# Middle attention by halves of four heads: scores and turned probabilities in alternation

## Chip, cores and metric

The kernel runs on one core of one Trainium2 chip. The metric is the device time of one execution in microseconds; the time of a kernel is the median of several runs, and one further execution is profiled.

## What is computed

The reference is a two-layer network on a batch of 2 sequences of 1024 tokens with 256 channels. Each layer is a sum of conditioned blocks: an adapter and a recurrent mixing block, a mixture of experts, then an attention whose output conditions a second, local attention, and a gated feed-forward block. The change touches only the attention in the middle, `_L1_cond_ref`:

```python
Q, K, V = (proj(Wq, bq), proj(Wk, bk), proj(Wv, bv))      # 16 heads of 16 channels
s_scores = jnp.einsum('bhsd,bhskd->bhsk', Q, Kg) * scale  # Kg: K at 32 listed keys
s_scores = jnp.where(prior_index_mask[:Ss][None, None], s_scores, -inf)
sparse_out = jnp.einsum('bhsk,bhskd->bhsd', jax.nn.softmax(s_scores, axis=-1), Vg)
...
return out @ Wo.T + bo
```

Every query looks at 32 listed keys, which may repeat. All listed keys lie among the first 256, so the kernel computes full scores against 256 keys and adds the logarithm of how often each key is listed (`lc`), which comes to the same softmax.

## The kernel before

The code is written with a tile framework: the program says which engine computes what on which tile; the framework puts in the waits, hands out the buffers of each pool and sets the order in every engine's queue. In that order the place of a statement in the program is its priority, and an instruction that lacks a buffer lets later ones that are ready go first. So queues are not strictly in program order.

The middle attention is `cond1_near` (L1014). After the projections (`cond1_project`) it has 32 items: 2 batches, 4 pairs of query blocks of 128, 4 groups `g` of 4 heads. A group's four heads lie in the four strips of 32 partitions, 16 rows each. An item goes through three steps:

- `scores` (L1037): 8 matmuls (4 heads x 2 query blocks, row block outside, head inside) into four PSUM banks `ps0` to `ps3`, one for each head. Then for each head and block a reduction on VectorE (L1056) that adds `lc`, negates, writes `pe` to SBUF and leaves the row minimum in `nm`, and an exponential on ScalarE (L1066).
- `turn` (L1069): for each head four transposes on TensorE (L1075) into one of two PSUM banks `ptp`, and a copy to `pt` in SBUF: heads 0 and 2 on VectorE (L1078), heads 1 and 3 on ScalarE (L1080).
- `values` (L1086): first one step that is left over from earlier items (`later`: dividing by the softmax's sum and turning back, L981 to L993, or a piece of the output projection, L1008; two of them when more than four are left), then 8 matmuls (L1097) into bank `po` and a copy `aU` on ScalarE (L1104).

`staggered` (L70) runs the steps as a pipeline: in round i, `scores` of item i, `turn` of item i-1, `values` of item i-2. The eight PSUM banks are all in use: four `ps`, two `ptp`, one `po`, one `pa` for the left-over steps. In float32 a matmul is two passes, that is two weight loads and two matmul records in the profile, except for a transpose, which is one.

When the stage ends, the last output steps run, a branch on the data follows that leaves out `cond1_any`, and then the second attention loads its weights (`load_attn1`, L1229).

Of the kernel before, what the change touches and what calls it, by code (L numbers as in the profile page):

```python
# [9 lines left out]
F32 = mybir.dt.float32  # L10
# [8 lines left out]
P = 128  # L19
# [10 lines left out]
NEAR = 256  # L30
# [39 lines left out]
def staggered(items, *steps):  # L70

    for i in range(len(items) + len(steps) - 1):
        for j, step in enumerate(steps):
            if 0 <= i - j < len(items):
                step(items[i - j])
# [796 lines left out]
def combine(k, x, ys):  # L872

    nc, tc = k.nc, k.tc
    with tc.tile_pool(name="mog", bufs=4) as gp, tc.tile_pool(name="moq", bufs=2, space=PSUM) as pp:
        for b4 in range(NCK):
            po = [pp.tile([P, CK], F32, name=f"po{c}") for c in range(2)]
            for j in range(4):
                blk = b4 * 4 + j
                g = []  # L880
                for kk in range(2):
                    t = gp.tile([P, C], F32, name=f"g{kk}")
                    i = kk * NBLK + blk
                    nc.gpsimd.indirect_dma_start(
                        out=t[:],
                        out_offset=None,
                        in_=ys[:],
                        in_offset=bass.IndirectOffsetOnAxis(ap=k.gi[:, i : i + 1], axis=0),
                    )
                    g.append(t)  # L890
                o = gp.tile([P, C], F32, name="o")
                nc.vector.tensor_scalar_mul(o, g[0], k.cw[:, 0, blk : blk + 1])
                nc.vector.scalar_tensor_tensor(o, g[1], k.cw[:, 1, blk : blk + 1], o, ALU.mult, ALU.add)
                for c in range(2):
                    nc.tensor.transpose(po[c][:, j * P : (j + 1) * P], o[:, c * P : (c + 1) * P], k.ident)
            for c in range(2):
                ts = slice(b4 * CK, (b4 + 1) * CK)
                nc.vector.tensor_add(x[:, c, ts], x[:, c, ts], po[c])
# [73 lines left out]
def cond1_divide(k, sp, tp, aU, aT, qs):  # L972


    nc = k.nc
    a = sp.tile([P, 16, 16], F32, name="a")

    def divide():
        pa = tp.tile([P, 4, P], F32, name="pa")
        for g in range(4):  # L980
            nc.tensor.transpose(pa[:, g, :], aU[g], k.ident)  # L981
        p4 = pa.rearrange("p g (r d) -> p (g r) d", d=32)
        rd = sp.tile([P, 16], F32, name="rd")
        nc.vector.reciprocal(rd, p4[:, :, 16])
        nc.vector.tensor_mul(a, p4[:, :, 0:16], rd.unsqueeze(2).to_broadcast([P, 16, 16]))

    def back():
        pb = tp.tile([P, 4, P], F32, name="pa")
        a2 = a.rearrange("p h d -> p (h d)")
        for c in range(2):  # L990
            nc.tensor.transpose(pb[:, c, :], a2[:, c * P : (c + 1) * P], k.ident)
        for c in range(2):
            nc.vector.tensor_scalar_add(aT[:, c, qs], pb[:, c, :], k.vec("bv", c))  # L993

    return [divide, back]
# [18 lines left out]
def cond1_near(k, x, o, ys):  # L1014

    nc, tc = k.nc, k.tc
    nkb = NEAR // P  # L1020
    with tc.tile_pool(name="l1r", bufs=2) as rp:
        its = []
        with tc.tile_pool(name="l1a", bufs=2, space=PSUM) as pp:
            combine(k, x, ys)
            for b in range(B):
                qT = rp.tile([P, 4, S], F32, name="qT")
                kT = rp.tile([P, 4, NEAR], F32, name="kT")
                v = rp.tile([P, nkb, 16, 32], F32, name="v")
                aT = rp.tile([P, 2, S], F32, name="aT")
                cond1_project(k, x, b, pp, qT, kT, v, NEAR)  # L1030
                its += [dict(at=(b, q0, g), qT=qT, kT=kT, v=v, aT=aT) for q0 in range(0, 8, 2) for g in range(4)]
        with (
            tc.tile_pool(name="l1s", bufs=2) as sp,
            tc.tile_pool(name="l1p", bufs=1, space=PSUM) as pp,
        ):

            def scores(it):  # L1037
                b, q0, g = it["at"]
                ps = [pp.tile([P, 2, NEAR], F32, name=f"ps{i}") for i in range(4)]
                for j in range(2):  # L1040
                    for i in range(4):
                        hp = slice(32 * i, 32 * i + 16)
                        nc.tensor.matmul(  # L1043
                            ps[i][:, j, :],
                            lhsT=it["qT"][hp, g, (q0 + j) * P : (q0 + j + 1) * P],
                            rhs=it["kT"][hp, g, :],
                            start=True,
                            stop=True,
                        )
                it["pe"] = []  # L1050
                for i in range(4):
                    pe = sp.tile([P, 2, NEAR], F32, name="pe", bufs=10)
                    for j in range(2):

                        nm = sp.tile([P, 1], F32, name="nm", bufs=4)
                        nc.vector.tensor_tensor_reduce(  # L1056
                            out=pe[:, j, :],
                            in0=ps[i][:, j, :],
                            in1=k.lc[:, q0 + j, :],
                            scale=-1.0,  # L1060
                            scalar=3.0e38,
                            op0=ALU.add,
                            op1=ALU.min,
                            accum_out=nm,
                        )
                        nc.scalar.activation(pe[:, j, :], pe[:, j, :], AF.Exp, bias=nm, scale=-1.0)  # L1066
                    it["pe"].append(pe)

            def turn(it):  # L1069
                it["pt"] = []  # L1070
                for i, pe in enumerate(it["pe"]):
                    ptp = pp.tile([P, nkb, 2, P], F32, name="ptp", bufs=2)
                    for j in range(2):
                        for kb in range(nkb):
                            nc.tensor.transpose(ptp[:, kb, j, :], pe[:, j, kb * P : (kb + 1) * P], k.ident)  # L1075
                    pt = sp.tile([P, nkb, 2, P], F32, name="pt", bufs=8)
                    if i % 2 == 0:
                        nc.vector.tensor_copy(pt, ptp)  # L1078
                    else:
                        nc.scalar.copy(pt, ptp)  # L1080
                    it["pt"].append(pt)

            state = {}
            later = []

            def values(it):  # L1086
                b, q0, g = it["at"]
                for _ in range(2 if len(later) > 4 else 1):
                    if later:
                        later.pop(0)()  # L1090
                if g == 0:
                    state["aU"] = sp.tile([P, 4, 2, P], F32, name="aU")
                aU = state["aU"]
                po = pp.tile([P, 2, P], F32, name="po")
                for kb in range(nkb):
                    for i in range(4):
                        nc.tensor.matmul(  # L1097
                            po[32 * i : 32 * i + 32],
                            lhsT=it["v"][:, kb, 4 * g + i, :],
                            rhs=it["pt"][i][:, kb],  # L1100
                            start=kb == 0,
                            stop=kb == nkb - 1,
                        )
                nc.scalar.copy(aU[:, g], po)  # L1104
                if g < 3:
                    return
                for j in range(2):
                    qs = slice((q0 + j) * P, (q0 + j + 1) * P)
                    later.extend(cond1_divide(k, sp, pp, [aU[:, n, j, :] for n in range(4)], it["aT"], qs))
                if q0 == 6:  # L1110
                    later.extend(cond1_output(k, b, o, it["aT"], pp, "pa"))

            staggered(its, scores, turn, values)
            for step in later:
                step()

# [553 lines left out]
```

## Time and profile before

| what | value |
|---|---|
| median of 3 runs | 1792.74 us (1789.65 to 1792.97) |
| the profiled execution | 1785.95 us, span 1784.2 us |
| mean granted TensorE clock | 0.942 |
| middle attention's items, first reduction to that of the last item | 807.17 to 997.20 us |
| L1043 matmuls, busy | 512 records, 61.5 us |
| L1097 matmuls, busy | 512 records, 36.1 us |
| VectorE's copies L1078 | 64, 44.1 us |
| ScalarE's copies L1080 | 64, 36.8 us |

PE is TensorE's matmuls, PEld its weight loads, DVE is VectorE, ACT is ScalarE. A line of groups gives source line, engine, operation, tiles written and read, shape and count; then busy time and mean nanoseconds of one; then the idle time of the engine just before these instructions and what ended it. A line of the timeline gives start and length in microseconds, and in brackets how long the engine was idle and what ended that. Matmuls overlap, so the busy time of a group counts overlapping ones once.

### The profile page before, as it was taken

The numbers are of one execution on the slowest core, as the hardware profiler recorded it, in microseconds if no ns is written. First come the engines' busy times: TensorE is split into PE (matmuls) and PEld (weight loads), VectorE is DVE, ScalarE is ACT, GpSimd is POOL, SyncE is SP. The second block draws the span as 40 slices with busy tenths as digits, with TensorE's granted clock in tenths as the row PEclk, the third lists the DMA queues.
The fourth block names the chain that finished last, engine by engine and source line by source line (L and its number), as shares of the span: only waits on it lengthen the run. The fifth ranks groups of instructions, "written<-read, shape, count | busy, mean of one in ns | idle before, by whom it ended". The sixth has DMA issues, their size and how long they took to land. (4 is left out here: it accounts for less than half of the span.)

```text
span 1784.2 us, 27948 instructions
## 1 busy us (share of the span) xinstructions
PE 1617.0 (91%) x11226; PEld 1037.3 (58%) x11226; DVE 905.1 (51%) x2589; ACT 656.2 (37%) x1450; POOL 173.0 (10%) x154
## 2 busy tenths in 40 slices
PE   6798788999599999689998879999999999999978
PEld 3345776456365665345655434676776467677546
DVE  2543746997300000246787512776872277687444
ACT  2123023344212222006777411553653155465321
POOL 0351420034100000420000010000000000000001
PEclk9699799999799999798999889999999999999969
DMA  8000006001334320210000020000000000000001
GB/s 310 0 1 1 3 3 205 1 24 48 122 103 130 106 87 31 65 42 1 1 2 1 2 97 0 1 2 1 2 1 1 0 1 1 1 1 2 1 0 48
DMA packets 38271, 64.66 MB, mean 36 GB/s; under 512 B 6897, under 2 KB 31729, under 8 KB 35185
## 3 DMA queue, kind: packets, MB, share of 16 engines
q1 hardware_dynamic: 33970, 52.25, 8.7%
q0 software_dynamic: 3072, 8.39, 1.5%
q8 instruction: 93, 1.52, 0.4%
q10 hardware_dynamic: 1088, 2.10, 0.4%
q14 instruction: 48, 0.39, 0.1%
HBM read 43.86 MB, written 18.87 MB: 35 GB/s over the span
## 5 line engine op out<-in xcount | busy, mean ns | idle before, releaser
L1382 ACT ACTIVATE pe<-pe,nm 128x449 f32<-128x449 f32 (+1 forms) x256 | 162.8, 638 | 237.0 <-DVE nm L1372 236.9
L1397 PE MATMUL pt<-ident,pe 128*128 128x128 f32 x960 | 132.3, 279 | 2.4 <-DVE pe L1387 0.8
L1372 DVE CUSTOM_DVE_ANT_0 pe<-ps,wb 128x449 f32<-128x449 f32 (+1 forms) x224 | 127.4, 605 | 5.7 <-PE ps L1366 4.8
L859 PE MATMUL po<-w,h 128*128 128x256 f32 x512 | 118.2, 384 | 0.0
L851 PE MATMUL ph<-xt,w 128*128 128x512 f32 x256 | 113.7, 602 | 2.3 <-ACT xt L846 2.3
L1364 PE MATMUL ps<-kT,qT 64*128 64x384 f32 (+1 forms) x512 | 113.1, 508 | 2.2 <-DVE nm L1372 1.1
L1066 ACT ACTIVATE pe<-pe,nm 128x256 f32<-128x256 f32 x256 | 105.8, 495 | 20.8 <-DVE nm L1056 20.7
L1415 PE MATMUL py<-ptt,v 128*64 128x128 f32 x1408 | 111.2, 282 | 0.0
L1397 PEld LDWEIGHTS pt<-ident,pe 128*128 128x128 f32 x960 | 103.1, 141 | 13.7 <-PE ps L1366 4.1
L859 PEld LDWEIGHTS po<-w,h 128*128 128x128 f32 x512 | 95.3, 190 | 23.4 <-issue 11.8
L1056 DVE CUSTOM_DVE_ANT_0 pe<-ps,lc 128x256 f32<-128x256 f32 x256 | 91.5, 420 | 32.3 <-PE ps L1043 31.4
L805 DVE SCALAR_TENSOR_TENSOR lc<-iok,idx,lc 128x256 f32<-128x256 f32 x248 | 105.7, 475 | 0.3
L1387 DVE TENSOR_SCALAR pe<-pe,rd 128x449 f32<-128x449 f32 (+1 forms) x256 | 100.4, 435 | 4.3
L838 DVE SCALAR_TENSOR_TENSOR xe<-more,xe 128x256 f32<-128x256 f32 x32 | 13.4, 479 | 170.0 <-DMA xe<-xs 159.4
L1075 PE MATMUL ptp<-ident,pe 128*128 128x128 f32 x512 | 80.3, 293 | 14.6 <-DVE pt L1078 11.0
L1415 PEld LDWEIGHTS py<-ptt,v 128*64 128x64 f32 x1408 | 77.2, 136 | 23.3 <-issue 21.2
L1400 DVE COPY ptt<-pt 128x512 f32<-128x512 f32 (+1 forms) x128 | 83.6, 653 | 4.5 <-PE pt L1397 3.9
L1075 PEld LDWEIGHTS ptp<-ident,pe 128*128 128x128 f32 x512 | 57.3, 146 | 47.2 <-DVE pt L1078 23.2
L851 PEld LDWEIGHTS ph<-xt,w 128*128 128x128 f32 x256 | 48.5, 193 | 62.2 <-issue 55.4
L1288 PE MATMUL pq<-c,w1ak 128*128 128x512 f32 x128 | 61.3, 623 | 13.7 <-DMA w1ak<-in_w1a 12.9
L1402 ACT COPY ptt<-pt 128x512 f32<-128x512 f32 (+1 forms) x128 | 68.7, 537 | 4.2 <-PE pt L1397 4.2
L854 ACT ACTIVATE h<-ph,vecs 128x512 f32<-128x512 f32 x64 | 44.0, 687 | 70.2 <-PE ph L851 70.2
(311 smaller groups left out, 2737.0 us busy)
## 6 DMA issues: line engine op xcount, KB each, us to landing
w<-in_mw SPq DMA_DIRECT2D x16, 1024.0 KB, 6.0
xs<-z SPq DMA_DIRECT2D x8, 1024.0 KB, 9.8
xe<-xs SPq DMA_DIRECT2D x8, 512.0 KB, 7.0
more<-xs SPq DMA_DIRECT2D x8, 512.0 KB, 3.9
ys<-ye SPq DMA_DIRECT2D x8, 512.0 KB, 6.4
x<-in_xT ACTq DMA_DIRECT2D x4, 512.0 KB, 6.1
out_x<-o SPq DMA_DIRECT2D x4, 512.0 KB, 2.9
w1c<-in_w1c SPq DMA_DIRECT2D x1, 1536.0 KB, 7.1
```

The lines of the kernel that those rows point to most:

```text
L805: nc.vector.scalar_tensor_tensor(n, key, k.idx[:, qb, j : j + 1], n, ALU.is_equal, ALU.add)
L851: nc.tensor.matmul(ph, lhsT=w1[:, c, m * P : (m + 1) * P], rhs=xt[:, c, :], start=c == 0, stop=c == 1)
L859: nc.tensor.matmul(po, lhsT=h[:, m, j * P : (j + 1) * P], rhs=w2[:, m, :], start=m == 0, stop=False)
L1056: nc.vector.tensor_tensor_reduce(out=pe[:, j, :], in0=ps[i][:, j, :], in1=k.lc[:, q0 + j, :], scale=-1.0, scalar=3.0e38, op0=ALU.add, op1= ...
L1066: nc.scalar.activation(pe[:, j, :], pe[:, j, :], AF.Exp, bias=nm, scale=-1.0)
L1075: nc.tensor.transpose(ptp[:, kb, j, :], pe[:, j, kb * P : (kb + 1) * P], k.ident)
L1364: nc.tensor.matmul(ps[:, i, 0:nk], lhsT=qs[i], rhs=kT[hp, m, k0 * P : k1 * P], start=True, stop=True)
L1372: nc.vector.tensor_tensor_reduce(out=pe, in0=ps[:, i, 0:W], in1=wl if n == NB - 1 else wb[:, P:] if n == 0 else wb, scale=-1.0, scalar=3.0e38,
L1382: nc.scalar.activation(pe, pe, AF.Exp, bias=nm, scale=-1.0, accum_out=den[:, i : i + 1])
L1387: nc.vector.tensor_scalar_mul(pe, pe, rd[:, i : i + 1])
L1397: nc.tensor.transpose(pt[:, j, :], it["pe"][i][:, j * P : (j + 1) * P], k.ident)
L1415: nc.tensor.matmul(py[64 * i : 64 * i + 64, m % 4, :], lhsT=v[:, k0 + j, hs] if j < nb else sv[:, hs], rhs=it["pt"][i][:, j, :], start=j == 0,
```

## The change

The loop is written out by hand with two halves in every round: for half 0 the scores of heads 0 and 1 of item i and the turning of heads 0 and 1 of item i-1, then the same for heads 2 and 3, then the values of item i-2. Banks, tiles, buffer counts and the engine of every operation stay as they are. `later` and `values` are untouched.

```diff
-            def scores(it):
+            def scores(it, half):
                 b, q0, g = it["at"]
-                ps = [pp.tile([P, 2, NEAR], F32, name=f"ps{i}") for i in range(4)]
+                heads = (2 * half, 2 * half + 1)
+                ps = {i: pp.tile([P, 2, NEAR], F32, name=f"ps{i}") for i in heads}
                 for j in range(2):
-                    for i in range(4):
+                    for i in heads:
                         hp = slice(32 * i, 32 * i + 16)
                         nc.tensor.matmul(
...
-                it["pe"] = []
-                for i in range(4):
+                pes = it.setdefault("pe", [])
+                for i in heads:
                     pe = sp.tile([P, 2, NEAR], F32, name="pe", bufs=10)
+                    pes.append(pe)
...
-            def turn(it):
-                it["pt"] = []
-                for i, pe in enumerate(it["pe"]):
+            def turn(it, half):
+                pts = it.setdefault("pt", [])
+                for i in range(2 * half, 2 * half + 2):
                     ptp = pp.tile([P, nkb, 2, P], F32, name="ptp", bufs=2)
                     for j in range(2):
                         for kb in range(nkb):
-                            nc.tensor.transpose(ptp[:, kb, j, :], pe[:, j, kb * P : (kb + 1) * P], k.ident)
+                            nc.tensor.transpose(ptp[:, kb, j, :], it["pe"][i][:, j, kb * P : (kb + 1) * P], k.ident)
...
-            staggered(its, scores, turn, values)
+            for i in range(len(its) + 2):
+                for half in range(2):
+                    if i < len(its):
+                        scores(its[i], half)
+                    if 0 <= i - 1 < len(its):
+                        turn(its[i - 1], half)
+                if i >= 2:
+                    values(its[i - 2])
```

More of the change, by code (lines that the diff above doesn't have):

```diff
@@ L1066, in scores @@
                         nc.scalar.activation(pe[:, j, :], pe[:, j, :], AF.Exp, bias=nm, scale=-1.0)
-                    it["pe"].append(pe)
-            def turn(it):
-                it["pt"] = []
-                for i, pe in enumerate(it["pe"]):
+            def turn(it, half):
+                pts = it.setdefault("pt", [])
+                for i in range(2 * half, 2 * half + 2):
                     ptp = pp.tile([P, nkb, 2, P], F32, name="ptp", bufs=2)
@@ L1080, in turn @@
                         nc.scalar.copy(pt, ptp)
-                    it["pt"].append(pt)
+                    pts.append(pt)
             state = {}
```

## The prediction

> **What bounds the kernel now.** I read the page's clock line first (one core, mean granted clock 0.942), then the costliest groups, then the timeline of the middle attention engine by engine, then its end. The groups say which work the change touches:
>
> ```profile
> L1066 ACT ACTIVATE pe<-pe,nm 128x256 f32<-128x256 f32 x256 | 105.8, 495 | 20.8 <-DVE nm L1056 20.7
> L1056 DVE CUSTOM_DVE_ANT_0 pe<-ps,lc 128x256 f32<-128x256 f32 x256 | 91.5, 420 | 32.3 <-PE ps L1043 31.4
> L1075 PE MATMUL ptp<-ident,pe 128*128 128x128 f32 x512 | 80.3, 293 | 14.6 <-DVE pt L1078 11.0
> ```
>
> Each engine sits waiting for another one: VectorE 31.4 us for scores, TensorE for VectorE's copies. In the timeline the first reduction of an item starts at 807.17 and that of the 32nd at 997.20; most of the 31 steps between take 5.76 us. One such step, TensorE's weight loads (each is followed at once by its matmul, so their starts show when a block of matmuls gives way to the next):
>
> ```profile
> 902.86 0.73 PEld L1043 LDWEIGHTS ps<-kT,qT 16*128 16x128 f32 x12 [0.17 <-issue]
> 903.92 0.86 PEld L1075 LDWEIGHTS ptp<-ident,pe 128*128 128x128 f32 x8 [0.33 <-issue]
> 904.74 0.47 PEld L981 LDWEIGHTS pa<-ident,aU 128*128 128x128 f32 x4
> 905.38 0.59 PEld L1097 LDWEIGHTS po<-pt,v 128*32 128x32 f32 x16 [0.17 <-issue]
> 906.38 0.29 PEld L1043 LDWEIGHTS ps<-kT,qT 16*128 16x128 f32 x2 [0.41 <-DVE nm L1056]
> 907.24 0.42 PEld L1075 LDWEIGHTS ptp<-ident,pe 128*128 128x128 f32 x4 [0.56 <-DVE pt L1078]
> 908.02 0.42 PEld L1075 LDWEIGHTS ptp<-ident,pe 128*128 128x128 f32 x4 [0.37 <-ACT pt L1080]
> 908.61 0.52 PEld L1043 LDWEIGHTS ps<-kT,qT 16*128 16x128 f32 x11 [0.17 <-issue]
> ```
>
> Block by block: scores of seven (head, row block) pairs 1.06, two turned heads and the divide step's four transposes 1.46, values 1.00, one lone score 0.86, third head 0.78, fourth head 0.59: 5.75 us. The two other engines in the same step:
>
> ```profile
> 903.73 0.42 DVE L1056 CUSTOM_DVE_ANT_0 pe<-ps,lc 128x256 f32<-128x256 f32 x1 [0.86 <-PE ps L1043]
> ...
> 906.49 0.69 DVE L1078 COPY pt<-ptp 128x512 f32<-128x512 f32 x1
> ...
> 907.93 0.69 DVE L1078 COPY pt<-ptp 128x512 f32<-128x512 f32 x1
> 909.50 0.42 DVE L1056 CUSTOM_DVE_ANT_0 pe<-ps,lc 128x256 f32<-128x256 f32 x1 [0.88 <-PE ps L1043]
> ```
>
> The loop is a ring. Eight reductions run 903.73 to 906.49 (0.345 each), only then does VectorE copy the first turned head (906.49); that frees a `ptp` bank, the third head is turned (907.24), the fourth after ScalarE's copy (908.02), and only behind these come the next scores (908.61), for which VectorE idles 0.88. VectorE has 4.8 us of work per step (8 x 0.345, two copies of 0.69, 0.66 for a divide step), ScalarE 4.75 (eight exponentials at 0.40, copies 0.56, 0.58, 0.36). Neither is the bound; the order is. What follows the stage (output steps, a branch, then the load of `w1ak` at 1035.12, from which the chain of waits goes on) starts when it ends, so a microsecond here is one of the span.
>
> **The change, part by part.** Instructions, shapes and copies stay the same in number; there is no DMA in the loop, and SP and POOL have nothing in it. What moves: two heads' scores, two heads turned, the other two heads' scores, the other two turned, values.
>
> (1) The ring is cut. VectorE's order becomes four reductions, copy, four reductions, copy. With the first half's scores starting at 0 on TensorE: reductions from 0.88 (902.86 to 903.73 now) to about 2.33 (the second row block's scores end 0.07 late), copy until 3.02; exponentials from 1.35, ScalarE's copy 2.97 to 3.53. TensorE: scores 0 to 1.06, heads 0 and 1 turned to 2.08, second scores to 3.14, third head at 3.14 (bank free at 3.02 + 0.05), fourth at 3.58 (free at 3.53 + 0.05). Nothing waits there. The new wait is the fourth head's: behind it on TensorE stand the values and the next scores, and its slack is nil.
>
> (2) The four heads lie in four row strips (16 of 32 rows each), and now four matmuls of one pass run at once. Now only two can. The rows:
>
> ```profile
> 906.38 0.69 PE L1043 MATMUL ps<-kT,qT 16*128 16x256 f32 x2
> 888.88 0.70 PE L1043 MATMUL ps<-kT,qT 16*128 16x256 f32 x4
> ```
>
> One matmul (two passes, x2) takes 0.69 and two heads together (x4) 0.70; single records in the block at 902.86 start in fours 7 ns apart and 0.216 us from four to four. So a half (four matmuls, two strips) needs the same four slots of 0.216 as the whole item does: 1.06 per half, 2.12 per item. Bounds: 0.63 (the lone score without its wait) if all four of a half went in two slots, 1.28 if the two heads were not paired; I take 1.06, the pair's row above.
>
> (3) TensorE's step then: scores 2 x 1.06; two heads and a change to scores 1.02 (0.59 for one at 908.02, plus four more at 0.109); two heads with a divide step 1.46 (with the shorter back step 1.25); values 1.00. Sum 5.60 or 5.39, mean 5.49: TensorE becomes the bound, 0.27 below 5.76, not the 0.95 that VectorE's 4.8 would allow.
>
> The Trainium skill, "TensorE: Matmul & The Clock Gate", section "Measured speedup vs the span model", gives 3.07 times for four row tiles, not the four of these records. By it splitting would lose only 2.8 slots, 0.60 us instead of 0.86, an estimate of 5.23 per step and some 7 us less than my sum; the trace decides.
>
> (4) The 31 steps. Sixteen of 5.76 with a divide or back step: -0.27 each, -4.3. Three without (from 826.84): 1.02 in place of 1.35 for the second pair of heads, so 5.16, -0.60 each, -1.8. Seven at the border of the two batches (5.99, 5.99, 7.15, 7.15, 9.07, 5.84, 6.19) have output steps between; I give them -0.27 too, -1.9 (bounds 0 and -4). Two steps (6.80, 6.75) fall on granted clock 0.50 from 844.4 to 847.8 and 868.3 to 871.7: a TensorE-bound step pays half of 3.4 us there, 7.2, so +0.9 (if the clock stays full: -2.6). The three first steps, 13.6 us at clock 0.50, pay for the doubled scores: +1.0 (bounds 0, as their scores already go one by one, and +2.7). Together -6.1 us.
>
> The same skill page, section "What's actually happening", says that the slow clock follows a window in which TensorE was idle. Here TensorE was busy 5.28 of the 6 us up to 844, so the rule does not explain the rows; if a fuller TensorE did keep the clock, it would give 3.5 us more.
>
> Span 1784.2 - 6.1 = 1778.1; the profiled execution took 1785.95 and lies 6.8 below the median, so against the runs 1792.74 - 6.1 = 1786.6, **1787**. What a measurement can tell from no change is about 0.2%, 3.6 us.
>
> **Rivals.** *Values torn apart (slower).* The queue is not in program order now: values and a lone score stand ahead of the third turned head because its bank is late, so a piece of work that is ready is put where a bank is missing. After the second scores that bank is free with 0.1 us to spare (3.02 against 3.14), for the fourth head with none. If the order on TensorE is made where it looks late, values go in between and are cut when it comes free. The end of the stage shows the price:
>
> ```profile
> 1003.47 0.57 PEld L1097 LDWEIGHTS po<-pt,v 128*32 128x32 f32 x10 [0.17 <-issue]
> 1004.45 0.85 PEld L1075 LDWEIGHTS ptp<-ident,pe 128*128 128x128 f32 x8 [0.41 <-issue]
> 1005.47 0.15 PEld L1097 LDWEIGHTS po<-pt,v 128*32 128x32 f32 x6 [0.17 <-issue]
> 1006.03 0.20 PEld L991 LDWEIGHTS pa<-ident,a 128*128 128x128 f32 x2 [0.41 <-issue]
> ```
>
> Values in two pieces cost 0.98 + 0.56 instead of 1.00, and a change more 0.15: 0.69 a step, 6.18 in all, +0.42 over 28 steps and the 1.9 of the slow clock: 1807. It decides above one cut of 0.27 per step; a cut in equal halves costs 0.29 and ends at 1795. For it: the cuts are there at the stage's end and in its first items. Against: the steady steps now hold their values whole.
>
> *The fourth head waits (no change).* If ScalarE has its `aU` copy (0.36) ahead of its first turned copy, TensorE waits about 0.32: 5.81 a step, about 1795; or both halves' scores stand together in the queue and the order is today's, 1793. Against: the aU copy belongs to values two items back, whose matmuls come late in the step.
>
> *VectorE becomes the bound (much faster).* If pairs cost no more slots, TensorE needs 4.43 (5.49 less one half's 1.06) and VectorE's 4.8 sets the step: -0.95 over 26 steps and little else, 1767. Against: the pair's row.
>
> **Numbers.** Forecast 0.45, values torn 0.35, no-change rival 0.13, much faster 0.07. Faster by over 0.2%: 0.37 of the forecast, 0.01 and 0.07, 0.45; within: 0.08 + 0.04 + 0.05 = 0.17; slower: 0.31 + 0.07 = 0.38. The forecast's own range is 1782 to 1791 (its bounds in (4)); the given one reaches to 1808 for torn values and to 1772 part of the way to the VectorE bound.
>
> **What would show it.** Right: steps of about 5.5 us; on TensorE scores in two blocks of 1.06 starting two at a time; reductions in fours; VectorE waiting some 0.8 for scores once a step. Wrong: L1097's blocks cut in two, turned heads waiting for ScalarE's copy, or steps below 5.2.

## The result, and the profile after

| | before | after |
|---|---|---|
| median | 1791.09 us (20 runs, 1784.22 to 1803.04) | 1791.3 us (20 runs, 1783.87 to 1806.23) |
| ratio of the times | | 1.001, 95% interval 0.9989 to 1.0031 |
| profiled execution | 1785.95 us, span 1784.2 | 1805.75 us, span 1804.0 |
| first reduction of the first item to that of the last | 190.03 us | 197.08 us |
| a steady step | 5.76 us (5.75 and 5.77 in turn) | 5.88 us (5.99 and 5.77 in turn) |

No difference that the measurement can tell. The two profiled executions lie 19.8 us apart, but most of that isn't the change. The windows view splits each span; its columns are the window, its length, busy time (and count) of PE, PEld, DVE, ACT and POOL, then the granted clock, DMA share and GB/s. Before:

```profile
0.00:807.17 807.17, 700.32 (x4618) 430.42 (x4618) 329.31 (x775) 198.43 (x323) 156.49 (x133) 0.92 0.21 71
807.17:997.20 190.03, 175.66 (x1532) 111.64 (x1532) 141.91 (x606) 146.14 (x342) 0.00 (x0) 0.95 0.01 1
```

And after:

```profile
0.00:819.79 819.79, 707.72 (x4618) 432.53 (x4618) 329.03 (x775) 198.42 (x323) 156.22 (x133) 0.91 0.21 70
819.79:1016.87 197.08, 191.55 (x1526) 124.89 (x1527) 141.45 (x606) 145.03 (x342) 0.00 (x0) 0.93 0.01 1
```

Ahead of the stage, where nothing was edited, the execution after has the same instructions (4618) at a lower clock and is 12.6 us longer. The 31 steps cost 7.05 us more; from the last item's reductions to the last output it is 27.8 us instead of 30.8, and behind that 3.1 us more. So the steps, not the totals of one execution, are compared below.

One steady step after, TensorE's weight loads in the timeline (start, length, in brackets the idle time before and what ended it):

```profile
882.76 0.73 PEld L1045 LDWEIGHTS ps<-kT,qT 16*128 16x128 f32 x8 [0.41 <-issue]
883.83 0.86 PEld L1077 LDWEIGHTS ptp<-ident,pe 128*128 128x128 f32 x8 [0.33 <-issue]
884.85 0.73 PEld L1045 LDWEIGHTS ps<-kT,qT 16*128 16x128 f32 x8 [0.17 <-issue]
886.16 0.42 PEld L1077 LDWEIGHTS ptp<-ident,pe 128*128 128x128 f32 x4 [0.58 <-DVE pt L1080]
886.73 0.42 PEld L1077 LDWEIGHTS ptp<-ident,pe 128*128 128x128 f32 x4
887.12 0.47 PEld L981 LDWEIGHTS pa<-ident,aU 128*128 128x128 f32 x4
887.76 0.59 PEld L1099 LDWEIGHTS po<-pt,v 128*32 128x32 f32 x16 [0.17 <-issue]
888.76 0.73 PEld L1045 LDWEIGHTS ps<-kT,qT 16*128 16x128 f32 x8 [0.41 <-issue]
```

The order is the one predicted, and the values are whole. But the second block of scores is followed only after 1.31 us (884.85 to 886.16) by the third head, which waits for VectorE's copy; the first block gives way after 1.07. VectorE in the same step:

```profile
884.04 0.42 DVE L1059 CUSTOM_DVE_ANT_0 pe<-ps,lc 128x256 f32<-128x256 f32 x1 [1.10 <-PE ps L1045]
...
885.42 0.69 DVE L1080 COPY pt<-ptp 128x512 f32<-128x512 f32 x1
...
887.51 0.69 DVE L1080 COPY pt<-ptp 128x512 f32<-128x512 f32 x1
```

The first reduction starts 1.28 us after its scores (882.76 to 884.04); the copy begins behind four reductions, at 885.42. The groups of the whole page:

```profile
L1059 DVE CUSTOM_DVE_ANT_0 pe<-ps,lc 128x256 f32<-128x256 f32 x256 | 93.7, 421 | 53.8 <-PE ps L1045 52.2
L1077 PEld LDWEIGHTS ptp<-ident,pe 128*128 128x128 f32 x512 | 58.6, 148 | 33.4 <-DVE pt L1080 16.3
```

VectorE now idles 52.2 us for scores (31.4 before). In the steady steps it waits 1.10 or 1.21 us for the first block of an item's scores, where it mostly waited 0.86 to 0.88; the rest of the difference lies in the first steps and at the border of the two batches. TensorE's weight loads wait 16.3 us for VectorE's copies (23.2 before).

### The profile page after: what moved, and what is told of

The parts are those of the page before. It is cut to its first block, busy times and chain, and to the rows that moved or that the text cites. A ratio compares the mean times of both kernels' runs of the same rounds, so it can differ in the third digit from the quotient of the medians.

```text
span 1804.0 us, 27949 instructions
## 1 busy us (share of the span) xinstructions
PE 1640.9 (91%) x11226; PEld 1053.3 (58%) x11226; DVE 904.5 (50%) x2589; ACT 655.1 (36%) x1450; POOL 172.8 (10%) x154
## 5 line engine op out<-in xcount | busy, mean ns | idle before, releaser
L1059 DVE CUSTOM_DVE_ANT_0 pe<-ps,lc 128x256 f32<-128x256 f32 x256 | 93.7, 421 | 53.8 <-PE ps L1045 52.2
L1045 PE MATMUL ps<-kT,qT 16*128 16x256 f32 x512 | 79.8, 426 | 1.8 <-DVE nm L1059 0.9
L1077 PEld LDWEIGHTS ptp<-ident,pe 128*128 128x128 f32 x512 | 58.6, 148 | 33.4 <-DVE pt L1080 16.3
L1298 PE MATMUL pq<-c,w1ak 128*128 128x512 f32 x128 | 61.5, 625 | 13.6 <-DMA w1ak<-in_w1a 12.8
```

Source lines behind the costliest of these rows:

```text
L1077: nc.tensor.transpose(ptp[:, kb, j, :], it["pe"][i][:, j, kb * P : (kb + 1) * P], k.ident)
L1298: nc.tensor.matmul(pq, lhsT=wk[:, c, ms], rhs=ci[:, c, ts], start=c == 0, stop=c == 1)
```

## Experiments

Lines are those of each kernel. "Items" is the time from the first item's first reduction to the last item's, "tail" from there to the end of the last output step. All medians are of runs on one chip together with the kernel before.

### 1. Copies between the reductions

```diff
                     if i < len(its):
                         scores(its[i], half)
+                        soften(its[i], 2 * half)
                     if 0 <= i - 1 < len(its):
                         turn(its[i - 1], half)
+                    if i < len(its):
+                        soften(its[i], 2 * half + 1)
```

`soften` is the second half of `scores`, reductions and exponentials, for one head.

> The changed kernel, but in each half VectorE's copy of a turned head comes after the third of its four reductions, and ScalarE's after the third of four exponentials, instead of behind the fourth. Matmuls and their order are the same. Theory (TensorE loses 0.25 us for VectorE's copy and 0.14 for ScalarE's in each step, because the first reduction starts 1.28 us after its scores and not 0.88): both copies end 0.3 to 0.4 earlier, both waits go, steps of 5.99/5.77 become about 5.60/5.39, the time falls by 9 to 12 us against the changed kernel, to 0.993 to 0.996 of the kernel before. Rival (the steps are long because TensorE's own work is longer than priced, and the waits are only where the slack shows): steps stay at 5.8 to 6.0, ratio to before 0.999 to 1.003.

Median 1786.72 us beside 1789.94, ratio 0.9973 (0.9953 to 0.9993). Steps 5.61 and 5.39. TensorE, one step:

```profile
903.88 0.73 PEld L1045 LDWEIGHTS ps<-kT,qT 16*128 16x128 f32 x8 [0.41 <-issue]
904.95 0.85 PEld L1081 LDWEIGHTS ptp<-ident,pe 128*128 128x128 f32 x8 [0.33 <-issue]
905.97 0.73 PEld L1045 LDWEIGHTS ps<-kT,qT 16*128 16x128 f32 x8 [0.17 <-issue]
907.03 0.86 PEld L1081 LDWEIGHTS ptp<-ident,pe 128*128 128x128 f32 x8 [0.33 <-DVE pt L1084]
907.86 0.47 PEld L981 LDWEIGHTS pa<-ident,aU 128*128 128x128 f32 x4
908.49 0.59 PEld L1103 LDWEIGHTS po<-pt,v 128*32 128x32 f32 x16 [0.17 <-issue]
909.49 0.73 PEld L1045 LDWEIGHTS ps<-kT,qT 16*128 16x128 f32 x8 [0.41 <-issue]
```

Both halves are now alike: 1.07 and 1.02, then 1.06 and 1.46 with the divide step, then 1.00; heads 2 and 3 go in one block of eight. No matmul was moved, so the 0.38 us per step are the two waits. The rival (TensorE's own work is longer than priced) falls with the steps. The ratio is a partial miss: 0.9973 lies between the theory's range and the rival's, and only its interval reaches into the theory's.

### 2. A ring of three banks

```diff
-                    ptp = pp.tile([P, nkb, 2, P], F32, name="ptp", bufs=2)
+                    ptp = pp.tile([P, nkb, 2, P], F32, name="ptp", bufs=3)
...
-        pa = tp.tile([P, 4, P], F32, name="pa")
+        pa = tp.tile([P, 4, P], F32, **ring)
...
-                    later.extend(cond1_output(k, b, o, it["aT"], pp, "pa"))
+                    later.extend(cond1_output(k, b, o, it["aT"], pp, dict(name="ptp", bufs=3)))
```

The back and output steps take `ring` in the same way; `ring` is `dict(name="ptp", bufs=3)` for all of them.

> The changed kernel, but the left-over steps' bank pa joins the two ptp banks: one ring of three banks for turned heads, divide, back and output steps (the same eight banks in all). Theory (waits for banks): the third head of an item finds a bank that has long been free, the fourth waits only for the copy two turns earlier; the 0.39 us of waits go, steps about 5.6/5.4, 8 to 12 us below the changed kernel, 0.993 to 0.996 of the kernel before. Rival (TensorE's own work): 5.8 to 6.0, ratio 0.999 to 1.003. A middle result (5.7) would mean that the divide steps, which now take a bank out of the ring, make a new wait.

Median 1780.36 us beside 1789.94, ratio 0.9938 (0.9914 to 0.9962). Steps 5.61 and 5.39 again, with no wait ahead of heads 2 and 3:

```profile
910.22 0.73 PEld L1045 LDWEIGHTS ps<-kT,qT 16*128 16x128 f32 x8 [0.17 <-issue]
911.28 0.85 PEld L1077 LDWEIGHTS ptp<-ident,pe 128*128 128x128 f32 x8 [0.33 <-issue]
```

VectorE's copy still comes behind four reductions here; only the bank is another. So a copy that is late by 0.3 us and a bank that is one too few are the two halves of one wait, and either cures it. The time fell by more than in experiment 1; most of that lies in the tail (see experiment 5).

### 3. Scores whole, the rest by halves

```diff
+                if i < len(its):
+                    scores(its[i])
                 for half in range(2):
                     if i < len(its):
-                        scores(its[i], half)
+                        soften(its[i], half)
```

`scores` issues the eight matmuls of an item, `soften` the reductions and exponentials of two heads.

> The changed kernel, but the eight score matmuls of an item are issued together over four row strips, as in the kernel before; reductions, exponentials and turned heads still go by halves. Theory (a half of two strips takes the four slots of a whole, so the split costs 1.06 us of TensorE per step): one block of 1.06 takes the place of 1.07 and 1.06, a value is put ahead of the third head, and the step falls to 5.0 to 5.2 us, 17 to 25 us below the changed kernel, about 0.987 to 0.991 of the kernel before. Rival (VectorE's chain sets the step, the doubled scores only fill its gaps): steps of 5.6 to 6.0, ratio above 0.995.

A miss: median 1796.76 us beside 1789.94, ratio 1.0025 (1.0004 to 1.0047), steps of 5.95. Both numbers are the rival's.

```profile
906.45 0.74 PEld L1044 LDWEIGHTS ps<-kT,qT 16*128 16x128 f32 x16 [0.41 <-issue]
907.53 0.85 PEld L1080 LDWEIGHTS ptp<-ident,pe 128*128 128x128 f32 x8 [0.33 <-issue]
908.35 0.25 PEld L991 LDWEIGHTS pa<-ident,a 128*128 128x128 f32 x2
908.77 0.14 PEld L1102 LDWEIGHTS po<-pt,v 128*32 128x32 f32 x2 [0.17 <-ACT pe L1072]
910.19 0.42 PEld L1080 LDWEIGHTS ptp<-ident,pe 128*128 128x128 f32 x4 [1.29 <-DVE pt L1083]
```

The theory's price of a block holds (all eight scores take 1.08, 906.45 to 907.53), but the gain of one block went into a longer wait: with all scores ready, five reductions stand ahead of VectorE's copy (909.45, 3.00 us after the scores start), and the third head waits 1.29 us. The step is the ring once more: 1.28 until the first reduction, 5 x 0.345, copy 0.69, heads three and four 0.63 + 0.58, the rest of the values 1.00: 5.90 of 5.95.

### 4. Head outside, row block inside

```diff
-                for j in range(2):
-                    for i in heads:
+                for i in heads:
+                    for j in range(2):
```

> The changed kernel, but in the scores the head is the outer loop and the row block the inner one, so neighbouring matmuls lie in the same strip and only the middle two of a half can pair. Theory (slots of 0.216 us for each pair, none shared within a strip): a half takes six slots, 1.49 us instead of 1.06, and a step 0.8 us more, 6.6 to 6.9, the whole some 25 us above the changed kernel; against that the first head's bank is full earlier, so VectorE's wait for scores falls below 1.1 us and the wait for its copy goes. Rival (it is the count of matmuls, not the pairing, that costs): blocks of 1.06, steps of 5.5 to 6.0.

One run: 1795.4 us, steps 5.99 and 5.77, the same as after and in the rival's range. The theory, that only neighbours pair, falls:

```profile
903.58 0.74 PEld L1045 LDWEIGHTS ps<-kT,qT 16*128 16x128 f32 x8 [0.41 <-issue]
904.65 0.86 PEld L1077 LDWEIGHTS ptp<-ident,pe 128*128 128x128 f32 x8 [0.33 <-issue]
```

The half takes 1.07 although both matmuls of a strip now stand next to each other. In the single records the first two passes start 13 ns apart (903.581 and 903.594), the next pair 0.320 us behind them and the others 0.215 apart; in the kernel after the first two start 7 ns apart. The records don't name a strip, so this is an inference from the starts: a matmul of the other strip isn't held up by the one ahead of it that waits for its own strip. Nor does the first head's bank fill earlier: the first reduction starts 1.27 us after the scores here too.

### 5. Whole scores and a ring of three, and the kernel before with the ring

Experiments 2 and 3 together, and the edit of experiment 2 alone on the kernel before.

> Scores of four heads in one block, softmax and turned heads by halves, and one ring of three banks for turned heads and left-over steps (the edits of the two runs before together). With whole scores alone the step rose to 5.95 us: VectorE put five reductions ahead of its copy and the third head waited 1.07 to 1.29 us for the bank. Theory (split scores cost TensorE one block of 1.06, and that run only hid the gain behind a bank wait): with a third bank the third head does not wait, the steps fall to 4.9 to 5.2 us, 0.986 to 0.990 of the kernel before. Rival (the split scores are not dearer, or VectorE's chain of some 4.8 us of work plus its wait for the scores sets the step): 5.5 to 6.0 us, 0.994 or more.

> The kernel before (scores of four heads, then the turned heads of the item ahead, then values), with the one change that pa joins the two ptp banks in a ring of three. Theory (what bounded the kernel before was the third head's wait for a bank, not the order of scores and turned heads): a third bank lets three heads be turned ahead of the reductions' end, the step falls from 5.76 to 5.2 to 5.5 us, 0.990 to 0.994 of the kernel before, better than or equal to the changed kernel with the same ring. Rival (the order is what bounds it, and halves are needed): 5.7 or more, 0.998 to 1.003.

The first: 1779.28 us beside 1791.09, ratio 0.9936 (0.991 to 0.9961), but steps of 5.96 and 5.73, so the theory fails: the steps are the rival's. The ratio lies just below the rival's 0.994, with the interval on both sides of it. The bank wait has moved from the third head to the fourth, behind the same five reductions:

```profile
906.53 0.74 PEld L1044 LDWEIGHTS ps<-kT,qT 16*128 16x128 f32 x16 [0.41 <-issue]
907.61 1.29 PEld L1080 LDWEIGHTS ptp<-ident,pe 128*128 128x128 f32 x12 [0.33 <-issue]
909.07 0.14 PEld L1102 LDWEIGHTS po<-pt,v 128*32 128x32 f32 x2 [0.17 <-issue]
910.28 0.42 PEld L1080 LDWEIGHTS ptp<-ident,pe 128*128 128x128 f32 x4 [1.07 <-DVE pt L1083]
```

The second: 1778.3 us beside 1791.09, ratio 0.992 (0.9891 to 0.9949), in the range the theory gave; but the steps (5.78 and 5.56) fell only 0.09 and not the 0.26 to 0.56 that it wanted. Three heads are turned ahead there; the fourth waits 0.57 us (at 909.22) for VectorE's copy, which still stands behind all eight reductions. Where, then, did both get their time? In the tail, which no expectation had:

| | items | tail | granted clock in the tail |
|---|---|---|---|
| before | 190.0 | 30.8 | 0.83 |
| after | 197.1 | 27.8 | 0.94 |
| 1, copies between | 183.4 | 28.0 | 0.88 |
| 2, after with ring | 182.6 | 22.6 | 0.92 |
| 3, scores whole | 193.2 | 28.7 | 0.88 |
| 5, scores whole with ring | 189.1 | 21.1 | 1.00 |
| 5, before with ring | 185.9 | 23.3 | 0.93 |

With a ring the tail is 21 to 23 us, without it 28 to 31 (us, one profiled execution each). Part of that is the clock. The kernel after and experiment 2 had the same 3.4 us at clock 0.50 in the tail, and differ by 5.2 us. The other tails without the ring in this table had 6.8 to 10.2 us at 0.50, the others with it none or 3.4; whether the waits in the tail bring the half clock on isn't shown. In the tail the output steps write `pa` in turn. ScalarE at full clock in the kernel before, with one bank, and in the last experiment below, with three:

```profile
1024.56 0.69 ACT L1009 ACTIVATE c<-pa,vecs 128x512 f32<-128x512 f32 x1 [2.07 <-PE pa L1008]
1027.32 0.69 ACT L1009 ACTIVATE c<-pa,vecs 128x512 f32<-128x512 f32 x1 [2.08 <-PE pa L1008]
```

```profile
1000.61 0.69 ACT L1009 ACTIVATE c<-ptp,vecs 128x512 f32<-128x512 f32 x1 [1.03 <-PE ptp L1008]
1002.33 0.69 ACT L1009 ACTIVATE c<-ptp,vecs 128x512 f32<-128x512 f32 x1 [1.03 <-PE ptp L1008]
```

With one bank matmuls and eviction take turns, 2.76 us a piece; with three they overlap, 1.72.

### 6. Without the alternation

```diff
                 for half in range(2):
                     if i < len(its):
                         scores(its[i], half)
+                for half in range(2):
                     if 0 <= i - 1 < len(its):
```

> The changed kernel without its alternation: scores of heads 0 and 1, scores of heads 2 and 3, then all four heads turned. Theory A (each strip works off its own matmuls, and later ones of other strips pass those that wait): the second half's matmuls run beside the first half's and both blocks together take 1.06 to 1.3 us, though eight matmuls stand in the same order as two halves. Theory B (matmuls start in the order of the queue, only neighbours pair): 1.9 us for both. In either case VectorE reduces all eight before its first copy, the third head waits for the bank and steps are 5.7 to 6.4 us.

One run: 1814.61 us, steps of 6.72, above the expected 5.7 to 6.4. VectorE makes all eight reductions before its first copy, and the third head waits 1.66 us:

```profile
904.68 0.76 PEld L1045 LDWEIGHTS ps<-kT,qT 16*128 16x128 f32 x16 [0.41 <-issue]
905.77 0.85 PEld L1077 LDWEIGHTS ptp<-ident,pe 128*128 128x128 f32 x8 [0.33 <-issue]
...
909.46 0.42 PEld L1077 LDWEIGHTS ptp<-ident,pe 128*128 128x128 f32 x4 [1.66 <-DVE pt L1080]
```

Theory A holds: both halves, side by side in the queue, take 1.09 us (904.68 to 905.77), 0.03 more than one half alone. So four strips take no longer than two for twice the work, and what the split costs is that each half stands alone, with transposes between.

### 7. Values between the turned heads

```diff
-                for half in range(2):
-                    if i < len(its):
-                        scores(its[i], half)
-                    if 0 <= i - 1 < len(its):
-                        turn(its[i - 1], half)
-                if i >= 2:
-                    values(its[i - 2])
+                if i < len(its):
+                    scores(its[i])
+                    soften(its[i], 0)
+                if 0 <= i - 1 < len(its):
+                    turn(its[i - 1], 0)
+                if i < len(its):
+                    soften(its[i], 1)
+                if i >= 2:
+                    values(its[i - 2])
+                if 0 <= i - 1 < len(its):
+                    turn(its[i - 1], 1)
```

Once with the banks of before, once with the ring of three.

> Scores of an item's four heads in one block; then reductions of heads 0 and 1, the two turned heads, reductions of heads 2 and 3, the left-over step and the values, and only then the other two turned heads; two ptp banks and one pa as in the kernel before. VectorE's order: five reductions, copy, three reductions, divide, copy. Theory (what the step pays for is TensorE's second block of scores and its waits for banks that VectorE's copies free; with neither, VectorE's own 4.8 us set the step): with scores at 0 on TensorE the copy ends at 1.28 + 5 x 0.345 + 0.69 = 3.69, the third head is due at 1.06 + 1.02 + 0.44 + 1.00 = 3.52, a wait of 0.2; the eighth reduction ends at 4.73, when the next scores are due; steps 4.8 to 5.0 us, 0.985 to 0.990 of the kernel before. Rival (some other delay of some 5.4 to 5.8 us per step is left whatever the order, for instance the wait of the next scores for the eighth reduction and then 1.28 us until VectorE can begin): 5.4 us or more, 0.992 or above.

> The run before (scores whole, values between the two pairs of turned heads, steps of 4.95 us) with pa joined to the two ptp banks in a ring of three. TensorE there still waits some 0.4 to 0.6 us per step for banks and VectorE only 0.29 to 0.39 for scores. Theory (VectorE's own work of 4.6 us, and the eighth reduction that frees the score banks, now set the step, TensorE's bank waits are slack): steps 4.8 to 5.0, the ratio to the kernel before within the earlier interval, 0.984 to 0.992. Rival (the bank waits still set it): steps 4.4 to 4.6, another 10 us, below 0.984.

Without the ring: 1772.33 us beside 1793.77, ratio 0.9881 (0.9843 to 0.9919), steps 4.95. With it: 1764.3 beside 1795.01, ratio 0.9831 (0.9799 to 0.9863), the fastest of all; steps 4.95 again, items 165.4 instead of 167.1, tail 21.6 instead of 31.9. So the second run has the steps that its theory gave and the ratio (below 0.984) of its rival; what is below comes from the tail, not from the steps. The intervals of the two runs overlap, and the tail's granted clock was 0.79 without the ring and 1.00 with it, so not all of those 10 us are the bank. One step with the ring:

```profile
871.62 0.74 PEld L1044 LDWEIGHTS ps<-kT,qT 16*128 16x128 f32 x16 [0.17 <-issue]
872.70 0.86 PEld L1080 LDWEIGHTS ptp<-ident,pe 128*128 128x128 f32 x8 [0.33 <-issue]
873.52 0.25 PEld L991 LDWEIGHTS ptp<-ident,a 128*128 128x128 f32 x2
873.94 0.59 PEld L1102 LDWEIGHTS po<-pt,v 128*32 128x32 f32 x16 [0.17 <-issue]
875.36 0.42 PEld L1080 LDWEIGHTS ptp<-ident,pe 128*128 128x128 f32 x4 [0.83 <-DVE pt L1083]
875.99 0.42 PEld L1080 LDWEIGHTS ptp<-ident,pe 128*128 128x128 f32 x4 [0.20 <-ACT pt L1085]
876.57 0.74 PEld L1044 LDWEIGHTS ps<-kT,qT 16*128 16x128 f32 x16 [0.17 <-issue]
```

Values (1.00 us) lie where TensorE would have waited. The theory's reason is not quite right: VectorE still waits 0.28 to 0.39 us per step, and the ring is closed over the copy as before, only shorter: 1.27 until the first reduction, 5 x 0.345, copy 0.69, then heads three and four 0.63 + 0.58, sum 4.90 of 4.95. The third bank doesn't help in the steps, since the divide step takes a place in the ring and the third head gets the first head's bank.

## Why the prediction was right and wrong

Predicted was 1787 us and faster by 6.1 us; measured is no change, 2.0 us less to 5.6 us more by the interval. The time lies in the range given, but that is in part luck: the range had been widened for two rivals, the forecast's own range of 1782 to 1791 ends at what was measured, and a gain of 6.1 us lies outside the interval. The mechanism failed at its first step.

**Step (1) failed, in one term.** It has "reductions from 0.88 (902.86 to 903.73 now)". Measured is 1.28. The 0.88 belongs to a block whose first scores had been done before:

```profile
900.40 0.30 PEld L1043 LDWEIGHTS ps<-kT,qT 16*128 16x128 f32 x4 [0.41 <-DVE nm L1056]
```

Of head 0 only the second row block was left at 902.86, and it stood in the first group of four, two passes deep. In a block that holds both row blocks of head 0 its strip has four passes, two slots of 0.216 more (0.43; measured 0.40). Both cases are there in the runs: in the steady steps the kernel after and all experiments on it have 1.27 to 1.28, and the kernel before with the ring, which keeps the lone score ahead, 0.90 (904.82 to 905.72). The kernel after has both by itself. At the border of the two batches it too does one score ahead:

```profile
935.82 0.29 PEld L1045 LDWEIGHTS ps<-kT,qT 16*128 16x128 f32 x2 [0.41 <-issue]
936.82 0.72 PEld L1045 LDWEIGHTS ps<-kT,qT 16*128 16x128 f32 x6 [0.17 <-issue]
938.90 0.73 PEld L1045 LDWEIGHTS ps<-kT,qT 16*128 16x128 f32 x8 [0.17 <-issue]
939.96 0.85 PEld L1077 LDWEIGHTS ptp<-ident,pe 128*128 128x128 f32 x8 [0.33 <-DVE pt L1080]
```

```profile
937.68 0.42 DVE L1059 CUSTOM_DVE_ANT_0 pe<-ps,lc 128x256 f32<-128x256 f32 x1
```

There the first reduction starts after 0.86 us (936.82 to 937.68), the second scores give way after 1.06 (938.90 to 939.96), and heads 2 and 3 go in one block, as predicted. The reduction of the first row block needs only two of the four passes but waits for the second row block, which is written into the same bank: in the single records of a steady step only the last pass of each head (883.518 and 883.524) gives the signal that VectorE waits for. The Trainium skill ("PSUM — Partial Sum Buffer", section "PSUM bank collisions raise a hardware error") says that VectorE must not read a bank while TensorE writes it, even in other columns; the 1.28 us agree with that, and no run here lets the two meet. Separate banks for the row blocks weren't tried: all eight are in use.

From there the working goes on as written, later: VectorE's copy ended at 3.35 instead of 3.02, the third head started at 3.40 instead of 3.14, ScalarE's copy was late too, and the step ended at 6.00 instead of 5.60. "Nothing waits there" and "slack nil" could not both be leaned on: a plan with 0.1 us to spare at one head and none at the next has no room for an error of 0.4 in its first line.

**Step (2) was right in the number**: 1.07 and 1.06 a half, busy time 79.8 us on L1045 (61.5 before). Its picture, matmuls that pair with their neighbours, was not: by experiments 4 and 6 each strip works off its own passes, the second 0.320 us after the first and the others 0.216 apart, whatever lies between. The 3.07 times of the Trainium skill for four row tiles ("TensorE: Matmul & The Clock Gate", section "Measured speedup vs the span model", there with K=32 and N=512) isn't what these strips do: 16 passes in four strips take 1.09, 8 in two 1.06. Three readings in the prediction were off, with nothing resting on them: the block at 902.86 holds six pairs (12 records) and not seven; by its own slots the bound for unpaired heads would be 1.06 + 4 x 0.216 = 1.92 and not 1.28; and ScalarE's terms add up to 4.70, not 4.75.

**Step (3)** held: 5.60 and 5.39 were TensorE's own work to 0.01 us, as experiments 1 and 2 show with 5.61 and 5.39. The step after had 0.38 more, the two waits.

**Step (4)** against the profiled pair, in us: the four first steps +4.2 (+0.4 predicted, +1.0 for three and -0.6 for the fourth; the clock stood at one half for 27.3 us from 820.4, before for 13.6 from 810.3); the next two, without left-over steps, -0.4 (-0.2 each, not -0.6); the twelve after them -0.6, of which the two half-clock steps of before, which weren't there after, are -2.0 (+0.9 predicted) and the rest +0.12 each (-0.27 predicted); the five at the border +2.2 and the last eight +1.6 (-0.27 each predicted). Sum +7.0. That the half-clock windows went as TensorE became fuller is what the Trainium skill's clock rule ("TensorE: Matmul & The Clock Gate", section "What's actually happening"), as the prediction quotes it, would make of it; in the kernel before with the ring one came back (917.1 to 923.9), and single executions can't settle whether that is cause or chance.

**Rivals.** *Values torn apart* did not happen in this kernel's steps; in the steady steps of experiments 3 and 5 with whole scores (2 and 14 loads) and 6 (10 and 6) the values are torn, and there TensorE waits 1.07 us or more for a bank. *The fourth head waits (no change)* came nearest in time, 1793 or 1795, and was right that a `ptp` bank is waited for; but the third head waits first, and for VectorE's copy, and `aU` stands behind ScalarE's turned copies, not ahead of them. *VectorE becomes the bound* was nearly right that 4.8 us were within reach, as experiment 7 shows with 4.95, but by another order than this change's.

Where the expected gain went: the ring was cut as meant, the scores took two blocks of 1.06 us a step as priced, and the 0.27 left over were more than eaten by 0.38 of waits for two banks, which came from a first reduction that starts 0.40 later.

## What to carry to other kernels

A latency read from one block holds only for what that block contains: count, for the very bank that the consumer waits on, how many passes its own strip has before it, and carry an error of that size through every slack in the plan. When a producer's work is put into more, smaller blocks, ask what the consumer's first wait becomes, and put work that needs none of the late banks (here the values) where one will be late, rather than hoping the copy is in time. A buffer that serves two stages, as `pa` does for the loop and for the output steps behind it, may cost more behind the loop than in it: 5.2 us of tail where the half clock was alike (after and experiment 2), against nothing in the steps of experiment 7.

## What the hardware showed that was not expected

By their starts, matmuls in different row strips don't keep the queue's order among themselves: a half whose two strips come one after the other in the program (experiment 4) took 1.07 us as an alternating one did, and two halves in sequence ran side by side in 1.09 (experiment 6), the second half's strips starting 26 ns after the first's (904.687 and 904.713) though the first half's second row blocks stand between. That the queue does hold them in the program's order is read from the gaps: 20 ns between the second start and the third here, where the kernel before, with its four heads side by side, has 7.
